# A two-layer attention and mixture-of-experts kernel: expert-owned table rows, routing by groups of tiles, and attention units in pairs

## The chip, the cores and the metric

The kernel runs on one core of one Trainium2 chip. The metric is the device time of one execution in microseconds (us). The core has a matrix engine (TensorE, "PE"; its weight loads are shown apart as "PEld"), a vector engine (DVE), a scalar engine (ACT), a general engine (POOL), and a sync engine (SP) that here only issues transfers. Each engine works through its own list of instructions in order, and waits on semaphores for the others.

## The reference, cut to what matters

All data is fp32. The input is x (8 batches of 100 tokens, width 512) and a context (8 batches of 722 rows, width 512). Two layers follow each other, each a cross attention and a mixture of eight experts.

```python
x = x + L0_xattn(layernorm(x), ctx)   # 16 heads of 32, causal: only context rows 0..99 count
x = x + L0_ffn(layernorm(x))          # gate over 8 experts, top 2, GELU, 512 -> 2048 -> 512
x = x + L1_xattn(layernorm(x), ctx)   # 16 heads of 64; keys and values: own 100 tokens and 722 context rows
x = x + L1_ffn(layernorm(x))          # router over 8 experts, top 2, SwiGLU, 512 -> 1024 -> 512, layernorm of the sum
```

In L1_xattn the keys and the values of the context are the same projection, `memories @ Wm`:

```python
mem = split_heads(memories @ Wm)
k = concatenate([k, mem], axis=2); v = concatenate([v, mem], axis=2)
out = einsum(softmax(einsum(q, k) * scale), v)
```

An expert computes only the tokens that chose it: a token has two experts, so each layer sends 1600 rows to experts.

## The kernel before, in words

The 800 tokens lie in seven tiles of 128 rows, the last of 32. The stages run one after the other, PE first in each.

**Weights.** The class `Weights` (L44-64) streams 1 MB pieces through a pool of eight buffers, in a fixed order, all on SP's queue; `get(k, ahead)` asks for piece k and lets later ones start.

**a0, the first attention.** 32 units, one for each of four column chunks and eight batches; projections of the next chunk's columns stand between the units, so the last chunk's eight units have none. While it runs, SP fills two DRAM tables, `sent` and `answers`, with zeros in pieces of 512 KB. Then an output loop over the seven tiles adds the projection to x, normalises each tile, and computes its router logits (`logits0`).

**Routing of the first layer.** After the last tile's logits `two_largest` (L188) finds both experts of all tokens at once, and `places` (L218) ranks the tokens for each expert by a matmul with a triangle of ones. It sorts the experts by their number of tokens into eight slots with capacities of 256 to 176 rows. Since a slot's rows start at a fixed place, a token's row is known only when all totals are known. `send` (L303-308) then issues 14 indirect DMAs on POOL (7 tiles, 2 experts each) that write rows of x into `sent`. While they run, `project_early` (L435) computes five units' context projections of the second attention (batch 0) and stores them in DRAM: `context_columns` (L406-415) makes `mT` by 16 matmul instructions, and `context_rows` (L417) transposes it to `mv`.

**FFN0.** Per slot, `arrived` (L322-329) reads up to 256 rows from `sent`, transposes them, `hidden0` (L656) and `products` (L341) multiply, `returned` (L353-363) writes rows to `answers`.

**Between the layers.** PE first projects five early units of batch 1; then POOL fetches two answers for each tile (`fetch`, L315), the sum is made, and after that the tiles are normalised and transposed one by one (a second loop), and q, k and v are multiplied (L400, L813).

**a1, the second attention.** 64 units: a unit is one batch b and one pair of heads ic. In unit n, PE projects the context for the unit (`keys` and `values`; a kept unit reloads it from DRAM on SP's queue instead), computes scores (`weighed`, L752), turns unit n-1's probabilities (`turned`, L773-779) and multiplies them with the values (`attended`, L794). DVE takes the row maximum (L756), ACT the exponential with its sum (L758), DVE the reciprocal of the sums (L763). POOL copies that to a [100,128] tile `wide` (L782), PE transposes it (L788), ACT copies the transpose, and DVE multiplies with it (L797).

**Output and routing of the second layer.** After the last unit: seven output projections (L840, L843), then normalisation (L118-140), transposes (L151) and logits (L166) of the seven tiles, then `two_largest`, `places` and 14 sends as before, the reading from `sent` (L329), and FFN1 (L884). The kernel ends with 14 fetches, a weighted sum, the layernorm and the store.

Of the kernel before, what the change touches and what calls it, by code (L numbers as in the profile page):

```python
# [13 lines left out]
P = 128  # L14
# [17 lines left out]
EARLY = ((0, 1, 3, 5, 7), (0, 1, 3, 5, 7))  # L32
KEPT = {(b, ic): (b * len(EARLY[0]) + k) for b in range(len(EARLY)) for k, ic in enumerate(EARLY[b])}


CAPS = (256, 240, 228, 220, 204, 200, 184, 176)
STARTS = tuple(sum(CAPS[:s]) for s in range(NE))
CAP = CAPS[0]
OVER = NT - CAPS[-1]
ROWS = sum(CAPS) + NE * OVER  # L40
# [3 lines left out]
class Weights:  # L44


    def __init__(self, nc, pool, pieces):
        self.nc, self.pool, self.pieces, self.tiles = nc, pool, pieces, []

    def load(self, n, behind=None):  # L50

        while len(self.tiles) < min(n, len(self.pieces)):
            t = self.pool.tile([P, 4, 512], F32, tag="w", name=f"w{len(self.tiles)}")
            piece = self.pieces[len(self.tiles)]
            if behind is not None:
                self.nc.gpsimd.tensor_copy(t[:1, 0, :1], behind[:1, 0, :1])
            self.nc.sync.dma_start(out=t, in_=piece() if callable(piece) else piece)
            self.tiles.append(t)
# [7 lines left out]
def two_layers(ctx: ExitStack, tc: tile.TileContext, a: dict, out: bass.AP):  # L66
# [8 lines left out]

    pieces = [a[n] for n in ("k_w", "q_w", "v_w", "o_w")]
    W_L0F = len(pieces)
# [8 lines left out]
    pieces += [a["Wq"][g] for g in range(2)] + [a["Wkv"][g] for g in range(4)]  # L86
    pieces += [a["Wm"][g] for g in range(2)] + [a["Wo"][g] for g in range(2)]
# [74 lines left out]
    def router_logits(lg, i, xT, wg, bg, psum, tag):  # L162
        w, t0 = rows[i], i * P
        ps = psum.tile([P, NE], F32, tag=tag, name="ps_lg")
        for dc in range(DC):
            nc.tensor.matmul(  # L166
                ps[:w], xT[:, dc, t0 : t0 + w], wg[:, dc, :], start=dc == 0, stop=dc == DC - 1 and bg is None
            )
        if bg is not None:
            nc.tensor.matmul(ps[:w], ones[:, :w], bg, start=False, stop=True)  # L170
        nc.vector.tensor_copy(lg[:w, i, :], ps[:w])

    def over_experts(t):
        return t.unsqueeze(2).to_broadcast([P, NTILE, NE])

    def largest(v, pool, name):

        m = pool.tile([P, NTILE], F32, tag=f"m_{name}", name=f"m_{name}")
        nc.vector.tensor_reduce(m, v, AX.X, ALU.max)
        at = pool.tile([P, NTILE, NE], F32, tag=f"at_{name}", name=f"at_{name}")  # L180
        nc.vector.tensor_tensor(at, v, over_experts(m), ALU.is_equal)
        nc.vector.tensor_tensor(at, at, rank.unsqueeze(1).to_broadcast([P, NTILE, NE]), ALU.mult)
        first = pool.tile([P, NTILE], F32, tag="first", name=f"first_{name}")
        nc.vector.tensor_reduce(first, at, AX.X, ALU.max)
        nc.vector.tensor_tensor(at, at, over_experts(first), ALU.is_equal)
        return m, at

    def two_largest(v, below, pool, name):  # L188
        m1, at1 = largest(v, pool, f"{name}1")
        rest = pool.tile([P, NTILE, NE], F32, tag="rest", name=f"rest_{name}")  # L190
        nc.vector.scalar_tensor_tensor(rest, at1, below, v, ALU.mult, ALU.add)
        m2, at2 = largest(rest, pool, f"{name}2")
        return m1, at1, m2, at2
# [8 lines left out]
    places_of = const.tile([P, 3, NE], F32, name="places_of")  # L202
    count = const.tile([P, NE], F32, name="count")
    for s in range(NE):
        nc.vector.memset(count[:, s : s + 1], float(s))
        for k, n in enumerate((STARTS[s], CAPS[s], sum(CAPS) + s * OVER - STARTS[s] - CAPS[s])):
            nc.vector.memset(places_of[:, k, s : s + 1], float(n))

    def row_of(s, r):
        return STARTS[s] + r if r < CAPS[s] else sum(CAPS) + s * OVER + r - CAPS[s]  # L210

# [3 lines left out]
    kept_keys = dram.tile([len(KEPT), P, S], F32, name="kept_keys")  # L215
    kept_values = dram.tile([len(KEPT), P, NSC, P], F32, name="kept_values")

    def places(at1, at2, pool, psum, tag, name):  # L218

        sel = pool.tile([P, NTILE + 1, NE], F32, tag="sel", name=f"sel_{name}")  # L220
        nc.vector.memset(sel[:, NTILE - 1 :, :], 0.0)
        nc.vector.tensor_tensor(sel[:, : NTILE - 1, :], at1[:, : NTILE - 1, :], at2[:, : NTILE - 1, :], ALU.add)
        nc.vector.tensor_tensor(
            sel[:LAST, NTILE - 1, :], at1[:LAST, NTILE - 1, :], at2[:LAST, NTILE - 1, :], ALU.add
        )
        before = pool.tile([P, NTILE + 1, NE], F32, tag="before", name=f"before_{name}")
        nc.vector.memset(before[:, 0, :], 0.0)
        for i in range(NTILE):
            nc.vector.tensor_tensor(before[:, i + 1, :], before[:, i, :], sel[:, i, :], ALU.add)
        ps = psum.tile([P, NTILE + 1, NE], F32, tag=tag, name=f"ps_rank_{name}")  # L230
        nc.tensor.matmul(ps, every, before, start=True, stop=False)
        nc.tensor.matmul(ps, upper, sel, start=False, stop=True)
        tot = ps[:, NTILE, :]
        square = [P, NE, NE]
        key = pool.tile([P, NE], F32, tag="key", name=f"key_{name}")
        nc.vector.scalar_tensor_tensor(key, tot, float(NE), rank, ALU.mult, ALU.add)
        hot = pool.tile(square, F32, tag="hot", name=f"hot_{name}")
        nc.vector.tensor_tensor(
            hot, key.unsqueeze(1).to_broadcast(square), key.unsqueeze(2).to_broadcast(square), ALU.is_gt
        )  # L240
        slot = pool.tile([P, NE], F32, tag="slot", name=f"slot_{name}")
        nc.vector.tensor_reduce(slot, hot, AX.X, ALU.add)
        nc.vector.tensor_tensor(
            hot, slot.unsqueeze(2).to_broadcast(square), count.unsqueeze(1).to_broadcast(square), ALU.is_equal
        )
        three = [P, 3, NE, NE]
        wide = pool.tile(three, F32, tag="wide", name=f"wide_{name}")
        nc.vector.tensor_tensor(
            wide, hot.unsqueeze(1).to_broadcast(three), places_of.unsqueeze(2).to_broadcast(three), ALU.mult
        )  # L250
        mine = pool.tile([P, 3, NE], F32, tag="mine", name=f"mine_{name}")
        nc.vector.tensor_reduce(mine, wide, AX.X, ALU.add)
        all_ = [P, NTILE, NE]
        over = pool.tile(all_, F32, tag="over", name=f"over_{name}")
        nc.vector.tensor_tensor(over, ps[:, :NTILE, :], mine[:, 1:2, :].to_broadcast(all_), ALU.is_ge)
        nc.vector.tensor_tensor(over, over, mine[:, 2:3, :].to_broadcast(all_), ALU.mult)
        where = pool.tile(all_, F32, tag="where", name=f"where_{name}")
        nc.vector.tensor_tensor(where, ps[:, :NTILE, :], mine[:, 0:1, :].to_broadcast(all_), ALU.add)
        nc.vector.tensor_tensor(where, where, over, ALU.add)
        out = []  # L260
        for k, at in enumerate((at1, at2)):
            pick = pool.tile([P, NTILE, NE], F32, tag="pick", name=f"pick{k}_{name}")
            nc.vector.tensor_tensor(pick, at, where, ALU.mult)
            place = pool.tile([P, NTILE], F32, tag="place", name=f"place{k}_{name}")
            nc.vector.tensor_reduce(place, pick, AX.X, ALU.add)
            whole = pool.tile([P, NTILE], mybir.dt.int32, tag=f"whole{k}", name=f"whole{k}_{name}")
            nc.vector.tensor_copy(whole, place)
            out.append(whole)
        who = pool.tile(square, F32, tag="who", name=f"who_{name}")
        nc.vector.tensor_tensor(  # L270
            who, hot.rearrange("p e s -> p s e"), count.unsqueeze(1).to_broadcast(square), ALU.mult
        )
        first = pool.tile([P, NE], F32, tag="firsts", name=f"firsts_{name}")
        nc.vector.tensor_reduce(first, who, AX.X, ALU.add)
        experts = pool.tile([P, NE], mybir.dt.int32, tag="experts", name=f"experts_{name}")
        nc.vector.tensor_copy(experts, first)
        much = pool.tile([P, NE], F32, tag="much", name=f"much_{name}")
        nc.vector.tensor_tensor(much, tot, mine[:, 1, :], ALU.is_gt)
        most = pool.tile([P, 1], F32, tag="most", name=f"most_{name}")
# [725 lines left out]
```

## Time and profile before

| what | value |
|---|---|
| median of three runs | 1883.63 us (1882.03 to 1885.28) |
| the profiled execution | 1887.75 us |
| its span | 1886.0 us |
| mean TensorE clock granted | 0.952 of full speed |
| PE busy | 1744.2 us, 92% of the span |
| DVE, ACT, POOL busy | 576.5, 468.3, 161.7 us |
| moved by DMA | 225.15 MB, mean 119 GB/s |

The profile is one execution; "busy" is the time in which an engine had an instruction at work. The stages lie in its span as follows, in us: a0 from 0 to about 170, its outputs and the logits to 207, routing to 255, FFN0 to 640, between the layers to 698, the products of q, k and v and the attention units to 1448, outputs and routing to 1550, FFN1 and the end to 1886. In tables by window, each engine has its busy time and, in parentheses, its number of instructions; then come the granted clock, the share of busy DMA engines and the GB/s. A time line row gives start, duration, engine, line, operation and tiles, and in brackets the idle time before it with what ended it.

### The profile page before, as it was taken

The numbers are of one execution on the slowest core, as the hardware profiler recorded it, in microseconds if no ns is written. First come the engines' busy times: TensorE is split into PE (matmuls) and PEld (weight loads), VectorE is DVE, ScalarE is ACT, GpSimd is POOL, SyncE is SP. The second block draws the span as 40 slices with busy tenths as digits, with TensorE's granted clock in tenths as the row PEclk, the third lists the DMA queues.
The fourth block names the chain that finished last, engine by engine and source line by source line (L and its number), as shares of the span: only waits on it lengthen the run. The fifth ranks groups of instructions, "written<-read, shape, count | busy, mean of one in ns | idle before, by whom it ended". The sixth has DMA issues, their size and how long they took to land. (4 is left out here: it accounts for less than half of the span.)

```text
span 1886.0 us, 26129 instructions
## 1 busy us (share of the span) xinstructions
PE 1744.2 (92%) x10442; PEld 1318.2 (70%) x10442; DVE 576.5 (31%) x1379; ACT 468.3 (25%) x1389; POOL 161.7 (9%) x281
## 2 busy tenths in 40 slices
PE   5999969999999879999999999999999939999990
PEld 2455559999999745666666666666666428999990
DVE  4465300101111140355444234444443321111115
ACT  2374311111111141343333323333332010010110
POOL 4010110000000130000000000000000140000003
PEclk9997879999999979999999999999999859999995
DMA  9701284464556552032000000000000056555523
GB/s 368 313 24 55 108 317 164 177 248 174 201 205 231 196 176 79 24 95 72 1 32 1 32 1 32 1 33 1 1 1 1 12 199 224 183 181 203 206 89 113
DMA packets 51883, 225.15 MB, mean 119 GB/s; under 512 B 8336, under 2 KB 10008, under 8 KB 35104
## 3 DMA queue, kind: packets, MB, share of 16 engines
q1 hardware_dynamic: 32440, 169.51, 24.8%
q0 software_dynamic: 10064, 32.15, 4.8%
q10 hardware_dynamic: 9240, 21.65, 3.2%
q8 instruction: 86, 1.41, 0.3%
q14 instruction: 53, 0.43, 0.1%
HBM read 176.76 MB, written 46.53 MB: 118 GB/s over the span
## 5 line engine op out<-in xcount | busy, mean ns | idle before, releaser
L341 PE MATMUL ps_y<-h,w 128*128 128x256 f32 (+7 forms) x1536 | 280.5, 344 | 0.0
L411 PE MATMUL ps_m<-cb,w 128*128 128x361 f32 x864 | 277.6, 472 | 0.0
L341 PEld LDWEIGHTS ps_y<-h,w 128*128 128x128 f32 x1536 | 268.6, 190 | 7.9
L411 PEld LDWEIGHTS ps_m<-cb,w 128*128 128x128 f32 x864 | 158.9, 189 | 95.4 <-issue 3.6
L656 PE MATMUL ps_h<-xgT,w 128*128 128x256 f32 (+7 forms) x1024 | 189.9, 347 | 0.0
L656 PEld LDWEIGHTS ps_h<-xgT,w 128*128 128x128 f32 x1024 | 181.0, 192 | 6.0
L758 ACT ACTIVATE pr<-ps_sc,m 100x822 f32<-100x822 f32 x128 | 120.0, 943 | 192.6 <-DVE m L756 192.6
L774 DVE COPY prT<-ps_ptA 128x500 f32<-128x500 f32 x128 | 82.2, 678 | 197.1 <-PE ps_ptA L773 197.1
L756 DVE TENSOR_REDUCE m<-ps_sc 100x1 f32<-100x822 f32 x128 | 123.8, 1009 | 47.2 <-PE ps_sc L752 47.2
L660 ACT ACTIVATE h<-ps_h,s_b 128x256 f32<-128x256 f32 (+7 forms) x128 | 56.2, 439 | 315.6 <-PE ps_h L656 315.6
L415 ACT COPY mT<-ps_m 128x361 f32<-128x361 f32 x128 | 59.0, 462 | 252.1 <-PE ps_m L411 224.3
L400 PE MATMUL ps_col<-xT,w 128*128 128x400 f32 x320 | 115.3, 519 | 0.0
L884 PE MATMUL ps_g<-xgT,w 128*128 128x256 f32 (+7 forms) x512 | 104.6, 348 | 0.0
L884 PE MATMUL ps_u<-xgT,w 128*128 128x256 f32 (+7 forms) x512 | 103.1, 344 | 0.0
L400 PEld LDWEIGHTS ps_col<-xT,w 128*128 128x128 f32 x320 | 61.9, 197 | 46.2 <-issue 4.6
L884 PEld LDWEIGHTS ps_g<-xgT,w 128*128 128x128 f32 x512 | 91.4, 192 | 3.0
L884 PEld LDWEIGHTS ps_u<-xgT,w 128*128 128x128 f32 x512 | 91.1, 191 | 2.8
L752 PE MATMUL ps_sc<-mT,qT 64*100 64x311 f32 (+1 forms) x512 | 91.9, 466 | 0.0
L889 ACT ACTIVATE sg<-ps_g 128x256 f32<-128x256 f32 (+7 forms) x64 | 22.3, 349 | 239.3 <-PE ps_g L884 239.3
L782 POOL COPY wide<-sums 100x128 f32<-100x128 f32 x64 | 18.8, 294 | 728.1 <-DVE sums L763 728.1
L890 DVE TENSOR_TENSOR h<-ps_u,sg 128x256 f32<-128x256 f32 (+7 forms) x64 | 24.4, 381 | 184.2 <-PE ps_u L884 152.9
L794 PE MATMUL ps_av<-prT,mv 128*64 128x100 f32 (+1 forms) x1536 | 80.6, 253 | 0.0
(240 smaller groups left out, 1964.0 us busy)
## 6 DMA issues: line engine op xcount, KB each, us to landing
w<-in_W SPq DMA_DIRECT2D x64, 1024.0 KB
w<-in_w_gate SPq DMA_DIRECT2D x16, 1024.0 KB
w<-in_w_up SPq DMA_DIRECT2D x16, 1024.0 KB
w<-in_w_down SPq DMA_DIRECT2D x16, 1024.0 KB
sent<-nil SPq DMA_DIRECT2D x25, 512.0 KB
cb<-in_ctxT ACTq DMA_DIRECT2D x8, 1444.0 KB
answers<-nil SPq DMA_DIRECT2D x19, 512.0 KB
xg<-sent POOLq DMA_DIRECT2D x18, 256.0 KB, 4.8
```

The costliest lines, as they stand in the source:

```text
L341: nc.tensor.matmul(py[:, k, :n], ws[f // 4][:, f % 4, dc * P : (dc + 1) * P], h[:, f, :n], start=f == 0, stop=f == nf - 1,)
L400: nc.tensor.matmul(ps[:, :HALF], w[c // 4][:, dc, (c % 4) * P : (c % 4 + 1) * P], xT[:, dc, cols], start=dc == 0, stop=dc == DC - 1,)
L411: nc.tensor.matmul(pm[:, : S // 2], w_m[ic // 4][:, dc, (ic % 4) * P : (ic % 4 + 1) * P], cb[:, dc, h * (S // 2) : (h + 1) * (S // 2)], st ...
L415: nc.scalar.copy(mT[:, h * (S // 2) : (h + 1) * (S // 2)], pm[:, : S // 2])
L656: nc.tensor.matmul(ph[:, :n], w[:, dc, j * P : (j + 1) * P], xg[:, dc, :n], start=dc == 0, stop=dc == DC - 1,)
L660: nc.scalar.activation(h[:, f, :n], ph[:, :n], AF.Gelu, bias=b1s[:, e, f : f + 1])
L752: nc.tensor.matmul(sc[:, bank, c0:c1], qT[r, ic, q0 : q0 + T], keys_, start=True, stop=True)
L756: nc.vector.tensor_reduce(m, sc[:, :, :NKH], AX.XY, ALU.max, negate=True)
L758: nc.scalar.activation(pr.rearrange("p (a n) -> p a n", a=2), sc[:, :, :NKH], AF.Exp, bias=m, accum_out=sums[:, j : j + 1],)
L774: nc.vector.tensor_copy(prT[:, : NSC - 1, :], pt)
L794: nc.tensor.matmul(po[r, 0, :], vj, prT[j][:w, c, :], start=c == 0, stop=c == NSC)
L884: nc.tensor.matmul(p_[:, :n], w_[:, dc, j * P : (j + 1) * P], xg[:, dc, :n], start=dc == 0, stop=dc == DC - 1,)
```

## The change

Six things are changed at once.

1. **Rows of the tables.** Each expert owns 800 rows of `sent` and `answers`: a token's row is expert times 800 plus its rank. A table has 6400 rows in place of 6700, and both are zero-filled whole, in 50 pieces (before, the main part of `answers` was left out: 44 pieces). The slots read their expert's rows by an address from a register, which POOL loads as well as SP.
2. **Routing by groups.** A class `Route` chooses, ranks and sends by groups of tiles: (0-2), (3-4), (5-6) in the first layer, (0-1), (2-3), (4), (5-6) in the second. `order()` sorts the experts into slots after the last group. One group's work is about 20 short DVE instructions, two rank matmuls and two sends for each tile.
3. **Early projections.** 14 units are kept in place of ten: all eight of batch 0, six of batch 1. Those of batch 0 are a generator of 24 steps: one step in each of the last ten iterations of a0's loop, six in its output loop, eight after `order()`. Wm and the context for them come through the weight pool ahead of the zero fill of `answers`. In the second attention the kept units are reloaded on POOL's queue.
4. **Between the layers.** Each tile is normalised and transposed as soon as its answers are added, in one loop. The weight order is Wq, Wm, Wkv, Wo.
5. **Attention units in pairs.** Units of batches 0 and 2, then of 1 and 3, alternate (kept, not kept); batches 4 to 7 follow in order. `wide` and its transposes are gone: SP writes the reciprocals to DRAM (100x2 numbers, transposed) and reads them back twice, spread over 64 partitions each. The multiply (L822) is placed one unit later on DVE, right behind the next unit's reciprocal (L787) and ahead of its copies of turned probabilities (L802).
6. **Outputs within the attention.** Output projection, normalisation, logits and the group's routing of tiles 0 to 4 are placed after units 33, 35, 37, 50 and 58; those of tiles 5 and 6 follow the last unit.

```diff
-EARLY = ((0, 1, 3, 5, 7), (0, 1, 3, 5, 7))
+EARLY = ((0, 1, 2, 3, 4, 5, 6, 7), (0, 1, 3, 5, 6, 7))
-ROWS = sum(CAPS) + NE * OVER
+ROWS = NE * NT
+GROUPS = ((0, 3), (3, 5), (5, NTILE)), ((0, 2), (2, 4), (4, 5), (5, NTILE))
...
+        def group(self, i0, i1, xn):
+            g, v = i1 - i0, self.logits[:, i0:i1, :]
+            at1 = self.largest(v, self.m[0][:, i0:i1], 1)
...
+            at2 = self.largest(other, self.m[1][:, i0:i1], 2)
...
+            nc.tensor.matmul(ps[:, : g + more, :], every, self.before[:, i0 : i1 + more, :], start=True, stop=False)
+            nc.tensor.matmul(ps[:, :g, :], upper, self.sel[:, i0:i1, :], start=False, stop=True)
+            row = self.temp([P, NTILE, NE], "row")[:, :g, :]
+            nc.vector.tensor_tensor(row, ps[:, :g, :], base.unsqueeze(1).to_broadcast([P, g, NE]), ALU.add)
...
+            for i in range(i0, i1):
+                for k in range(2):
+                    d = nc.gpsimd.indirect_dma_start(
+                        out=sent, out_offset=bass.IndirectOffsetOnAxis(ap=self.where[k][: rows[i], i : i + 1], axis=0),
+                        in_=xn(i)[: rows[i], :], in_offset=None,
+                    )
...
+    def rows_of(table, layer, s, r, n):
+        of_all = table.rearrange("(e r) d -> e r d", e=NE)
+        return of_all[bass.ds(owner[layer][s], 1), r : r + n, :].rearrange("o r d -> (o r) d")
...
-            nc.gpsimd.dma_start(out=xg[:w, s, :], in_=sent[row : row + w, :])
+            nc.gpsimd.dma_start(out=xg[:w, s, :], in_=rows_of(sent, layer, e, r0 + s * P, w))
...
+        fill(sent)
+        weights.load(W_L0F)
+        fill(answers)
...
         for n in range(len(units) + 2):
+            if n >= len(units) - B:
+                next(steps)
...
             if i > 0:
                 logits0(i - 1)
+                next(steps)
         logits0(NTILE - 1)
+        route.order(lambda: weights.load(W_L0F + 2))
+        for _ in steps:
+            pass
...
+            xn = fw.tile([P, D], F32, tag="y", name="xn1")
+            scaled(xn, x[:, i, :], *factors(moments(x[:, i, :], "a1"), "b", twice=True))
+            to_columns(xT1, xn, i * P, rows[i], ps, gamma1, beta1)
+            nc.gpsimd.tensor_tensor(x[:, i, :], x[:, i, :], bo, ALU.add)
...
-                nc.sync.dma_start(out=mT, in_=kept_keys[KEPT[b, ic]])
+                nc.gpsimd.dma_start(out=mT, in_=kept_keys[KEPT[b, ic]])
...
             nc.vector.reciprocal(sums, sums)
+            share, over = shares[b * IC + ic], aw.tile([P, T], F32, tag="share", name="over1", bufs=4)
+            nc.sync.dma_start(out=share.rearrange("j t -> t j"), in_=sums)
+            for r, j in zip(rows_, range(2)):
+                nc.sync.dma_start(out=over[r], in_=share[j].partition_broadcast(H1))
...
-            wide = small.tile([T, 2, H1], F32, tag="wide", name="wide1")
-            nc.gpsimd.tensor_copy(wide, sums.unsqueeze(2).to_broadcast([T, 2, H1]))
...
-            nc.tensor.transpose(po[:, 1, :], wide.rearrange("t j d -> t (j d)"), ident[:T, :T])
...
-            nc.scalar.copy(over, po[:, 1, :])
-            nc.vector.tensor_tensor(qT[:, ic, b * T : (b + 1) * T], po[:, 0, :], over, ALU.mult)
+            mine = qT[:, ic, b * T : (b + 1) * T]
+            nc.scalar.copy(mine, po)
+            return lambda: nc.vector.tensor_tensor(mine, mine, over, ALU.mult)
...
+        units = [(b + 2 * k, ic) for b in range(2) for ic in range(IC) for k in range(2)]
+        units += [(b, ic) for b in range(4, B) for ic in range(IC)]
...
+            if divide is not None:
+                divide()
+            if before is not None:
+                divide = attended(*before[:4], *turn)
+            before = here
+            if n in due:
+                output(due[n])
+        divide()
+        attended(*before[:4], *turned(*before[4]))()
+
+        for i in range(NTILE):
+            if i not in due.values():
+                output(i)
+        route.order(lambda: weights.load(W_L1F + 2))
```

## The prediction

> **What bounds the kernel now.** I read the page first: busy shares, then the slices in tenths.
>
> ```profile
> PE 1744.2 (92%) x10442; PEld 1318.2 (70%) x10442; DVE 576.5 (31%) x1379; ACT 468.3 (25%) x1389; POOL 161.7 (9%) x281
> ...
> PE   5999969999999879999999999999999939999990
> ...
> PEclk9997879999999979999999999999999859999995
> ```
>
> TensorE (PE) is the bound. 1886.0 - 1744.2 = 142 us of the span are PE idle, in few places: the start, slices 5 and 6 (routing), 13 and 14 (between the layers), 32 and 33 (second routing), the end. Work that moves between other engines counts only there; elsewhere only PE work that vanishes counts. Next, windows of 20 us at those places and inside the attention:
>
> ```profile
> 240.00:260.00 20.00, 7.64 (x23) 6.24 (x24) 2.64 (x8) 1.76 (x2) 5.74 (x14) 0.50 0.78 292
> 680.00:700.00 20.00, 8.80 (x31) 6.24 (x32) 8.04 (x21) 11.36 (x35) 8.72 (x7) 0.58 0.15 51
> 1000.00:1020.00 20.00, 20.00 (x152) 13.56 (x151) 9.14 (x18) 7.20 (x22) 0.59 (x2) 1.00 0.00 1
> 1520.00:1540.00 20.00, 0.31 (x2) 0.12 (x1) 3.57 (x22) 0.00 (x0) 12.47 (x13) 0.50 0.64 239
> ```
>
> PE is solid at 1000-1020 and nearly empty at 1520-1540, with the clock at half. The time line there names the holder, POOL's sends, one each 1.28 us, and the chain of waits goes on to FFN1:
>
> ```profile
> 1523.88 1.02 POOL L308 DMA_INDIRECT sent<-xnf,whole_f  x1 [11.94 <-DVE pick_f L263]
> ...
> 1540.41 0.86 POOL L308 DMA_INDIRECT sent<-xnf,whole_f  x1 [0.30 <-issue]
> ```
>
> ```profile
> 1543.20 2.91 DMA xg<-sent
> ...
> 1550.00 2.13 PE ps_g L884 x5
> ```
>
> From the last send's end (1541.27) to FFN1 (1550.00) are 8.73 us. In the attention, POOL's `wide` copies date the reciprocals, and the PE rows price what goes:
>
> ```profile
> 839.19 0.29 POOL L782 COPY wide<-sums 100x128 f32<-100x128 f32 x1 [11.78 <-DVE sums L763]
> 846.18 0.29 POOL L782 COPY wide<-sums 100x128 f32<-100x128 f32 x1 [6.70 <-DVE sums L763]
> 853.97 0.29 POOL L782 COPY wide<-sums 100x128 f32<-100x128 f32 x1 [7.49 <-DVE sums L763]
> 937.88 0.29 POOL L782 COPY wide<-sums 100x128 f32<-100x128 f32 x1 [9.93 <-DVE sums L763]
> 948.10 0.29 POOL L782 COPY wide<-sums 100x128 f32<-100x128 f32 x1 [9.92 <-DVE sums L763]
> ```
>
> ```profile
> 1002.93 0.31 PE L788 MATMUL ps_av<-ident,wide 100*128 100x100 f32 x1
> 1003.16 1.25 PE L794 MATMUL ps_av<-prT,mv 128*64 128x100 f32 x24
> ```
>
> A unit that is not kept takes 948.10 - 937.88 = 10.22 us. A kept one with one that is not takes 853.97 - 839.19 = 14.78, in steps of 6.99 and 7.79. So a kept unit costs 4.56, that is 5.66 us less. The transpose lasts 0.31 but holds the stream for about 0.2 (the next matmul starts 0.23 after it).
>
> **What the Trainium skill says.** "TensorE: Matmul & The Clock Gate", Part 1: after an idle window of some 3.4 us PE falls to half clock, and needs about as long busy to come back. The windows agree in kind (0.50 at 1520-1540, 1.00 at 1000-1020). The same page, "Architectural detail": ACT and DVE take their instructions strictly in order; so an early instruction that waits holds all behind it. The trace of before has no case that I rest on. "DMA: Bandwidth & Descriptors", "Anatomy of one DMA": about 2 us of each transfer are fixed, mostly the confirmation of the write; its rules for kernel authors say that a strided last dimension becomes one descriptor per element. The trace has only larger transfers (`back<-answers` 3.8 us median, `xg<-sent` 4.8), which lie above it.
>
> **The change part by part.** Sums are against the profiled execution (1887.75, span 1886.0, so 1.75 lies around it); the median is 1883.63, 4.1 lower, and I take the difference over.
>
> *First routing and its fill-ins.* Before: logits done 206.96, first FFN0 matmul 255.00, 48 us, of which five early units fill about 30. An early unit is some 5.9 us of PE (16 L411 matmuls 5.1, transposes 0.9). Ten of 24 steps go into a0's last iterations, 3 and a third units, 20 us; there PE is busy throughout but at clock 0.52, the units being chains of short work (3.03 us each, against about 2.8 with column matmuls between), so I take 9 as hidden: +12 (bounds 0 and +20). Six steps in the output loop, 11.7 us, in iterations whose PE is busy 4.65 of 5 us: +10 (+5 to +12). Groups' waits of DVE and rank matmuls: +3. Logits end at about 232. The last group then needs 2.8 (choice) + 0.7 (rank) + 2.6 (rows), four sends of 1.28 = 5.1, and 8.73 to FFN0: 20 us, in which the last eight steps (15.6) are hidden. FFN0 starts at 252: -3 (range -10 to +8), with three more units done. Filling 50 pieces in place of 44 adds 3 MB of SP transfers under a0; hidden, the DMA share there being low by 140 us, and if not, the context for the steps comes ahead of the second fill anyway. The stores' queue on SP holds nothing urgent but `order()`'s register loads, long after.
>
> *Address registers.* One more register operation on POOL for each of 36 row transfers: nothing under FFN0's solid PE, 0.3 us ahead of the first `xg`.
>
> *Between the layers.* Before, the last `ps_y` ends at 639, q's first matmul is at 697.84. Fetching ends at 673, then a second pass of seven tiles. With normalisation and transposes in the fetch loop, after the last fetch only one tile's chain (about 3 us for the sum and norm, 2 for transposes and copies, and 7 for weights and the start) is left: q at 685, -13 (-5 to -18). The sixth early unit lies in the wait for fetches. If the fetches are late, it is this chain that is late, equally.
>
> *Attention.* 64 transposes by 0.2 = -13 (0 to -15). Four more kept units by 5.66 = -22.6; their reloads pass from SP to POOL's queue, where nothing else stands in the attention but sends of groups. The second context of a pair is loaded when a buffer comes free, one unit ahead: +4 (0 to +5).
>
> *The new wait.* Reciprocal, write of 200 single numbers, read back, multiply. On SP the reads wait behind the write; on DVE the multiply stands behind the next unit's reciprocal; behind it are the copies of turned probabilities, for which PE's `attended` waits. No row shows such a transfer: from below twice 2 us = 4 us by the skill's price, an estimate; from above two of `xg<-sent`, 2 x 4.8 = 9.6. I take 6.5. It may last the spacing of reciprocals, 6.99 at the least, plus about 2 us of slack until the copies matter: 9. So nothing; at 9.6 it is 28 units by 0.6 = +17. With that cover gone each further us costs a us per unit.
>
> *Outputs and the second routing.* Before: 1448.4 (last `attended`) to 1550.0, 101.6 us. After, behind the last unit: output 5 6.4, norm 3.05 (from the matmul's end at 1454.72 through add, statistics, root, scaling), transposes and router 2.5; output 6 6.9, norm 3.05, 1.7; choice 3.4, rank and rows 2.1, four sends 5.1, 8.73 + 0.3: 43 us. In the attention, outputs 0 to 4: 5 x (6.9 + 1.7) + 3 x 0.7 = 45 us of PE, and waits, since PE meets the transposes two score products after the output: each 3.45 less what covers it, 17; rank matmuls wait for some 3.1 in two groups, 6; 1 more. 43 + 45 + 24 = 112 against 101.6: +11 (0 to +25; a falling clock after such waits is in the upper end). POOL's seven bias adds ahead of the last sends lie under the tail's chain.
>
> *FFN0, FFN1, tail.* Same instructions and sizes: 0.
>
> Sum: -3 - 13 - 13 - 22.6 + 4 + 11 = -36.6. In the profile 1887.75 - 36.6 = 1851; in the median 1883.63 - 36.6 = 1847.
>
> **The rivals.** *A, slower: the shares come too late.* If the round trip is 11 us, each pair takes 2 x (11 - 2) = 18 in place of 14.78 us: 14 pairs cost 45, more than all gains; median 1892. It decides from about 10.3 us, where the pairs cost 14 x 2.6 = 36. For it: single-number writes of which this profile has no measure, and a write that must be confirmed before each read. Against: the DMA share of 0.00 in the attention, so the queues are empty; and all shown transfers, much larger, take under 5.
>
> *B, the outputs' waits cost their double.* Each wait of 3 us and more lets the clock fall, and the next several us run at half: 5 x 4 = 20 more, median 1867. For it: 0.50 at 1500-1520, where just these norms and transposes run. Against: single waits of 3 us lie near the window's length.
>
> *C, the waits are covered.* Scores, context matmuls and other tiles cover the 24 us, and a0's steps fill only stretched time: -24, median 1823. For it: PE's clock of 0.52 in a0's tail, half of whose time could be taken without loss. Against: PE's order is fixed, and it meets the transposes early.
>
> *D, nothing is won in routing at all.* Early units merely move, and the first layer gives back +8 in place of -3, the gap between the layers -5: median 1866; it adds to B or A rather than deciding a sign.
>
> **How the numbers follow.** My own case, 1833 to 1866 and centred on 1847: 0.46. C, below: 0.11. B and D, up to 1880: 0.13. Within 0.2% (1879.9 to 1887.4, what this measurement can just tell from no change): 0.03. A, and any wait of its kind at the new places, above: 0.27. So faster 0.70, same 0.03, slower 0.27. The range, 1816 to 1898, leaves out some 0.05 below and 0.14 above, A's dearer half.
>
> **What would show it.** Right: L752 to L819 follow each other without L788's row; the spacing in pairs stays at about 14.4; DVE's row for L822 has little idle before it, put to a DMA; FFN0 starts at about 252, q about 12 us after the last fetch, and from the last `attended` to FFN1 are some 44 us. Wrong: L822 with hundreds of us of idle before it, and PE idle ahead of L819 (A); clock under 0.9 in the slices with outputs (B); FFN0 later than 260, which would mean that a0 hid nothing; or context matmuls that wait for `cb` at each new pair of batches.

## The result, and the profile after

The changed kernel is slower: a median of 1972.86 us in four runs (1962.4 to 1979.17) against 1882.83 in four runs of the kernel before; the ratio is 1.0471, with a 95% interval of 1.0423 to 1.0519. The forecast was 1847. The profiled execution is the shortest of the four, 1962.4 us with a span of 1960.9, so the times read from it lie some 10 us under the median. First its page, the same lines as shown of before:

```profile
PE 1755.8 (90%) x10398; PEld 1320.0 (67%) x10398; DVE 590.0 (30%) x1450; ACT 484.2 (25%) x1412; POOL 168.6 (9%) x263
...
PE   5999889999999789787998998999899939999990
...
PEclk9999889999999989898999898899899969999995
```

Counted from 0, there are new dips of PE where it was solid before: slices 16 to 18, 21, 24 and 28, all in the second attention, with a lower clock beside most of them. The old dips (5, 13, 14, 32) are still there. To see how much, I cut the span at five marks that both kernels have, and set the forecast's own steps beside them (us; the forecast is before plus the sum's terms for that stretch; e1, e4, e10 and e14b are experiments told below).

| stretch | before | forecast | after | e1 | e4 | e10 | e14b |
|---|---|---|---|---|---|---|---|
| start to the first FFN0 matmul | 255.0 | 252 | 253.7 | 253.7 | 250.4 | 253.8 | 254.0 |
| to the first q matmul | 442.8 | 430 | 444.2 | 443.1 | 443.5 | 443.1 | 442.6 |
| to the 32nd reciprocal (the paired units) | 370.1 | 345 | 408.7 | 344.1 | 344.6 | 344.1 | 338.3 |
| to the 64th reciprocal (single units, with outputs 0 to 4 where they are moved) | 377.0 | 440 | 456.2 | 461.3 | 442.9 | 377.6 | 370.0 |
| to the first FFN1 matmul | 104.9 | 46 | 59.5 | 58.4 | 49.6 | 97.8 | 99.7 |
| to the end of the span | 336.2 | 336 | 338.6 | 340.0 | 338.8 | 337.6 | 339.8 |

Of the 111 us between forecast and profile, 64 lie in the paired units, 16 in the stretch with the outputs, 14 between the layers, 13 behind the last unit, the small rest at the start and the end.

The view of waits by engine and line of the kernel after, limited to DVE, names a wait that the kernel before does not have (total us, number of times, longest). Limited to PE, it names what follows from it:

```profile
DVE qT L822 <- DMA over<-shares: 105.2, 31, 8.5
```

```profile
PE ps_mv L437 <- DVE prT L802: 40.5, 12, 5.6
```

Of the 105.2 us, 79.9 lie in the paired stretch.

SP's time line in the paired units shows where it comes from. L789 is the issue of a write of reciprocals, L791 the two reads, which SP may issue only when the write has landed:

```profile
854.99 0.28 SPq L789 DMA_DIRECT2D shares<-sums  x1
862.51 1.08 SPq L791 DMA_DIRECT2D over<-shares  x2
863.69 1.11 SPq L789 DMA_DIRECT2D shares<-sums  x1
871.16 1.08 SPq L791 DMA_DIRECT2D over<-shares  x2
873.65 0.28 SPq L789 DMA_DIRECT2D shares<-sums  x1
881.41 1.27 SPq L791 DMA_DIRECT2D over<-shares  x2
```

From the issue of a write to that of its reads are 7.5 to 7.8 us here (5.5 to 9.6 over the 32 paired units, 7.1 on average), and the write of the unit at 861.51 waits on SP behind the reads of the unit before. DVE and PE in the same place:

```profile
861.51 0.17 DVE L787 RECIPROCAL sums<-sums 100x2 f32<-100x2 f32 x1 [1.11 <-ACT pr L782]
866.60 0.26 DVE L822 TENSOR_TENSOR qT<-qT,over 128x100 f32<-128x100 f32 x1 [4.92 <-DMA over<-shares]
866.78 1.26 DVE L802 COPY prT<-ps_ptA 128x500 f32<-128x500 f32 x2
```

```profile
863.54 0.66 PE L437 MATMUL ps_mv<-ident,mT 128*128 128x128 f32 x4
867.50 0.44 PE L437 MATMUL ps_mv<-ident,mT 128*128 128x128 f32 x2 [3.31 <-DVE prT L802]
867.87 0.42 PE L776 MATMUL ps_sc<-kT,qT 64*100 64x100 f32 x4
868.13 2.21 PE L776 MATMUL ps_sc<-mT,qT 64*100 64x311 f32 x8
```

DVE has its reciprocal at 861.51 and then stands at the multiply L822 until 866.60; the copies L802, which it could have made from about 863 on (PE's transposes for them are done then), come after it; PE waits 3.31 us for them. Then the scores take 2.21 us in place of 1.39, at a granted clock of 0.60 (868.1 to 870.4). This is the chain that rival A described, at its place.

In the single units the write is faster, but not fast:

```profile
1303.38 0.28 SPq L789 DMA_DIRECT2D shares<-sums  x1
1308.71 1.08 SPq L791 DMA_DIRECT2D over<-shares  x2
```

It takes 5.3 us from issue to issue here, 5.8 in the median of the last 32 units. The units are 10.0 us apart, and the multiply finds its shares ready.

### The profile page after: what moved, and what is told of

It reads as the page before. It is cut to its first block, busy times and chain, and to the rows that moved or that the text cites. A ratio compares the mean times of both kernels' runs of the same rounds, so it can differ in the third digit from the quotient of the medians.

```text
span 1960.9 us, 26528 instructions
## 1 busy us (share of the span) xinstructions
PE 1755.8 (90%) x10398; PEld 1320.0 (67%) x10398; DVE 590.0 (30%) x1450; ACT 484.2 (25%) x1412; POOL 168.6 (9%) x263
## 4 chain that ended last, share of the span: by engine, by line
PE 42%; issue 34%; DMA 16%; DVE 4%; ACT 2%; SPq 1%; POOL 0%; POOLq 0%; another core or an unknown queue 0%; ACTq 0%; DVEq 0%
PE ps_m L425 13%; PE ps_col L414 7%; DMA answers<-y 6%; DMA shares<-sums 5%; PE ps_sc L776 3%; PE ps_v L847 3%; PE ps_av L819 3%; PE ps_o L865 2%; PE ps_mv L437 2%; PE ps_ptA L801 2%; DMA over<-shares 2%; PE ps_v L516 1%; DMA back<-answers,where 1%; PE ps_o L621 1%; ACT pr L782 1%
## 5 line engine op out<-in xcount | busy, mean ns | idle before, releaser
L425 PE MATMUL ps_m<-cb,w 128*128 128x361 f32 x896 | 307.0, 493 | 0.0
L425 PEld LDWEIGHTS ps_m<-cb,w 128*128 128x128 f32 x896 | 172.6, 199 | 102.8 <-issue 17.1
L802 DVE COPY prT<-ps_ptA 128x500 f32<-128x500 f32 x128 | 81.8, 677 | 149.6 <-PE ps_ptA L801 149.5
L819 PEld LDWEIGHTS ps_av<-prT,mv 128*64 128x64 f32 (+1 forms) x1536 | 74.7, 146 | 50.7 <-issue 48.5
L437 PE MATMUL ps_mv<-ident,mT 128*128 128x128 f32 (+1 forms) x384 | 64.0, 295 | 49.1 <-DVE prT L802 40.5
L776 PE MATMUL ps_sc<-mT,qT 64*100 64x311 f32 (+1 forms) x512 | 102.7, 517 | 0.0
L819 PE MATMUL ps_av<-prT,mv 128*64 128x100 f32 (+1 forms) x1536 | 88.4, 266 | 4.7 <-DVE prT L802 4.2
L437 PEld LDWEIGHTS ps_mv<-ident,mT 128*128 128x128 f32 (+1 forms) x384 | 41.6, 142 | 64.3 <-DVE prT L802 43.9
```

The source lines that it names most:

```text
L425: nc.tensor.matmul(pm[:, : S // 2], w_m[ic // 4][:, dc, (ic % 4) * P : (ic % 4 + 1) * P], cb[h][:, dc, : S // 2], start=dc == 0, stop=dc = ...
L437: nc.tensor.transpose(pt[:w, c - c0, :], mT[:, c * P : c * P + w], ident)
L776: nc.tensor.matmul(sc[:, bank, c0:c1], qT[r, ic, q0 : q0 + T], keys_, start=True, stop=True)
L802: nc.vector.tensor_copy(prT[:, : NSC - 1, :], pt)
L819: nc.tensor.matmul(po[r, :], vj, prT[j][:w, c, :], start=c == 0, stop=c == NSC)
```

## The experiments

My theory after the result: the share round trip makes the paired stretch long (A); the outputs inside the attention wait for their own norms and choice and pull the clock down (B). The rival to A was that the pairing itself does it: late contexts, or reloads on POOL's queue. The rival to B was that outputs are cheap there and only shares are at fault. In every verdict "before" is the kernel before on the same chip.

### e1: shares as before, all else changed

```diff
-            nc.sync.dma_start(out=share.rearrange("j t -> t j"), in_=sums)
-            for r, j in zip(rows_, range(2)):
-                nc.sync.dma_start(out=over[r], in_=share[j].partition_broadcast(H1))
-            return prs, over
+            return prs, sums
...
+            nc.gpsimd.tensor_copy(wide, sums.unsqueeze(2).to_broadcast([T, 2, H1]))
...
+            nc.tensor.transpose(po[:, 1, :], wide.rearrange("t j d -> t (j d)"), ident[:T, :T])
```

> The changed kernel with one part undone: the reciprocals are spread as before (POOL copy, PE transpose, multiply behind the value products), nothing goes through DRAM. If the share round trip is what stretched the paired units, the time from the first q matmul to the 32nd reciprocal falls from 408.7 to about 350 us, the single units cost 0.2 us more each again, and the whole comes to 1905 to 1925. If the outputs inside the attention or the pairing itself (contexts loaded late, reloads on POOL) hold it, the paired stretch stays near 400 and the whole above 1950.

Measured: 1900.89 us, ratio 1.0086 (1.0057 to 1.0115). The paired stretch is 344.1 us, its reciprocals 7.8 and 7.0 us apart as before. That is better than expected (about 350, and 1905 to 1925 for the whole). So the pairing, the late contexts and POOL's reloads cost nothing; with four more kept units the stretch is 26.0 us shorter than before, where 22.6 were forecast for them. The shares cost 65 us there. Windows over the paired stretch, of the changed kernel and of e1, show in what form:

```profile
697.87:1106.58 408.71, 363.51 (x2343) 229.75 (x2344) 136.33 (x249) 120.10 (x344) 22.35 (x42) 0.92 0.32 53
```

```profile
696.79:1040.93 344.14, 344.13 (x2374) 220.71 (x2375) 136.71 (x249) 120.19 (x344) 31.55 (x73) 0.99 0.19 59
```

PE idles for 45 us where e1 has no idle time at all, and it is busy 19 us longer though it makes 32 transposes less, at a clock of 0.92. The waits are two thirds of the cost; the slow clock behind them is the rest.

The five outputs cost as much as in the changed kernel: the stretch of single units is 461.3 against 377.6 in e10, which has none in it: 84 us.

### e2: the shares through DRAM in the kernel before

The same lines moved into the kernel before, with the multiply one unit later.

> The kernel before with one part done alone: reciprocals through DRAM, multiply one unit later. If the round trip is the cause, the units of batches 2 to 7 (10.22 us apart, more than a trip of 9.4) run without a wait at about 10.0, and only the 20 short spacings of batches 0 and 1 are stretched, by 2 to 4 us each second one: net 1875 to 1900. If the trip costs nothing by itself, the 64 transposes are simply gone: 1870. If SP or the DMA engines are slowed as a whole, every unit is longer than 10.2 and it is over 1910.

Measured: 1924.76 us, ratio 1.0223 (1.0204 to 1.0242). By its time that is the third case, over 1910; by its units it is the first, only dearer. The single units are 9.98 us apart, the 0.24 us of a transpose less, as expected. But the stretch of batches 0 to 3 takes 414.6 us against 370.1, with spacings up to 19.9 in batches 0 and 1. In this kernel the kept units' reloads stand on SP's queue too, behind reads that wait for writes, so that two waits add; I had not counted the queue. The run shows that the trip alone, on this queue, costs 44 us; it does not separate the two waits.

### e3 and e4: where the outputs stand

e3 is e1 with all seven projections behind the last unit and the rest tile by tile; e4 is e1 with an output in three steps:

```diff
-            if n in due:
-                output(due[n])
+            for k, step in enumerate((output, logits, grouped)):
+                if n - k in due:
+                    step(due[n - k])
```

> As e1_wide, and all seven output projections behind the last unit, followed by norms, logits and groups tile by tile. If the five outputs inside the attention cost their 86 us (measured in the changed kernel as longer spacings) mostly in waits, this is 35 to 55 us faster than e1_wide: 1860 to 1880. If the outputs inside the attention are cheap and only the shares were at fault, it is slower than e1_wide by 10 us or more.

> As e1_wide, but an output is cut in three: the projection with add and norm after its unit, transposes and logits after the next unit, choice, ranks and sends after the one behind that. The waits for the norm and the choice lie under a unit each. If the waits are the cost, each of the five outputs adds 8 to 10 us in place of about 17, the clock stays at 1.00 there, and the whole comes to 1860 to 1875, below e3. If the cost is the work itself or the clock, it stays within 10 us of e1_wide.

Measured: e3 1877.90 us, ratio 0.9975 (0.9963 to 0.9987); e4 1870.18, ratio 0.9933 (0.9909 to 0.9957). Both times lie within what was expected if B holds. But e3 gains 23 us on e1 and not 35 to 55: it wins 84 in the attention, and its end, tile by tile, is 64 us longer (122.0 against 58.4). PE's time line of e1 shows one output inside the attention:

```profile
1122.37 7.13 PE L865 MATMUL ps_o<-w,qT 128*128 128x512 f32 x16
1129.43 0.42 PE L776 MATMUL ps_sc<-kT,qT 64*100 64x100 f32 x4
1132.53 0.66 PE L157 MATMUL ps_tp<-ident,xnf 128*128 128x128 f32 x4 [2.68 <-DVE xnf L146]
1133.92 1.35 PE L173 MATMUL ps_lg<-p_w_router,xTf 128*128 128x8 f32 x8 [0.73 <-ACT xTf L159]
1138.31 0.58 PE L252 MATMUL ps_rank<-before,every 128*128 128x16 f32 x2 [3.04 <-DVE before L249]
1138.73 0.59 PE L253 MATMUL ps_rank<-sel,upper 128*128 128x16 f32 x2
1139.16 7.88 PE L425 MATMUL ps_m<-cb,w 128*128 128x361 f32 x16
```

The waits are 2.68 + 0.73 + 3.04 = 6.45 us. The granted clock is 0.50 from 1134.5, after the first two of them, to 1144.8, and the 16 context matmuls that follow take 7.88 us where they take 5.13 elsewhere: 2.75 us for the clock. In the changed kernel the window with an output at 1200 to 1220 has a clock of 0.75. Windows over the stretch of single units, of e1 and of e10, split the whole cost:

```profile
1040.93:1502.24 461.31, 437.43 (x2751) 280.37 (x2750) 177.62 (x395) 142.03 (x383) 19.22 (x42) 0.96 0.04 13
```

```profile
1041.06:1418.63 377.57, 376.62 (x2599) 247.10 (x2598) 154.30 (x297) 125.22 (x363) 9.39 (x32) 1.00 0.03 9
```

PE idles 23 us more with outputs than without, and is busy 61 us more. For 32 us of its busy time in e1 the clock stands at 0.50, which is worth 16; so the five outputs are 23 us of waits, 16 of slow clock and some 45 of work. In e4 PE works on a unit in between, and the stretch falls from 461.3 to 442.9, still 65 above e10: there 10 us are waits and 8 are the clock. What is left in e4 above the work is thus about half of what e1 had; an output costs 13.1 us and not the 8 to 10 that were expected.

### e5, e9 and e13b: what makes the write slow

e5 writes the same 200 numbers as 100 runs of two, read in the old places, so that shares come in a wrong order. e9 writes one head's 100 numbers singly and reads them for both heads. e13b lays them out token by token and reads both heads at once:

```diff
+            nc.sync.dma_start(out=share, in_=sums)
+            nc.sync.dma_start(out=over, in_=share.partition_broadcast(P))
...
+                for j in range(2):
+                    r = slice(j * H1, (j + 1) * H1)
+                    nc.vector.tensor_tensor(mine[r], mine[r], over[r, :, j], ALU.mult)
```

> The changed kernel, with the 100x2 reciprocals written as 100 runs of two numbers in place of 200 single ones (the reads are the same, so the shares come in a wrong order: the attention's weights are not the reference's). If the number of single runs sets the length of the write, the time from the write's issue to the reads' issue in the quiet units falls from 5.5 to 3.5 to 4.5 us, and the paired stretch from 408.7 to about 390, the whole to 1945 to 1960. If the time is a fixed latency, it stays at 5.5 and the whole at 1960 to 1980.

> The changed kernel, with the reciprocals of one head of the pair alone written (100 single numbers in place of 200) and read twice, so the second head is divided by the first one's sums: its output is not the reference's. If the number of runs is what the write takes its time for, its 5.5 us in quiet units fall to about 2.9 as with 100 runs of two, and the whole to about 1895. If the 4-byte size is what is slow, they fall to no less than 4.5, and the whole stays above 1920.

> The changed kernel, with the reciprocals of a unit laid out token by token in DRAM (100 runs of two numbers), read back by one transfer to all 128 partitions, and the multiply split in two by head. If the 4-byte runs of the write are the cause, the write takes about 2.9 us as in e5, the paired stretch from the first q matmul to the 32nd reciprocal is 340 to 350 us in place of 408.7, and the whole 1885 to 1900. If e5 was fast for its wrong order alone, or the larger read takes its place, it stays over 1920.

Measured: e5 1893.63 us, ratio 1.0048 (1.0031 to 1.0065), over 50 us less than expected, with a paired stretch of 342.0 in place of about 390. e13b 1889.96, ratio 1.0033 (1.0015 to 1.0052), as expected. SP's time line in single units, of e5, of e9 and of e13b:

```profile
1301.16 0.28 SPq L789 DMA_DIRECT2D shares<-sums  x1
1304.16 1.08 SPq L791 DMA_DIRECT2D over<-shares  x2
```

```profile
1299.65 0.28 SPq L789 DMA_DIRECT2D shares<-sums  x1
1305.19 1.08 SPq L791 DMA_DIRECT2D over<-shares  x2
```

```profile
1306.83 0.30 SPq L789 DMA_DIRECT2D shares<-sums  x1
1309.83 0.32 SPq L790 DMA_DIRECT2D over<-shares  x1
```

3.0, 5.5 and 3.0 us; in the median of the last 32 units 3.0, 5.9 and 3.0. A hundred single numbers take as long as two hundred (5.8), a hundred runs of two take 3.0: the number of runs is not what counts, the 4-byte run is. So the first of e9's two cases fell. (e9's whole time, 3168.39 us, ratio 1.6815 (1.6781 to 1.6848), says nothing on this: its wrong shares send so many rows to some experts that the overflow work of FFN1 runs, with 15326 PE instructions in place of 10398.) With pairs of numbers, e13b's waits for the shares fall from 105.2 to 22.8 us, and its paired stretch to 337.5, below e1's 344.1: of this trip PE feels nothing (it idles 0.1 us in the stretch), and the transposes are saved.

What I can't tell apart is whether a run of 4 bytes is slow as such, or because neighbouring ones lie side by side in DRAM; no run spread them out.

### e6 and e7: between the layers, and the last choice

e6 is e1 with batch 1's early stores issued by SP in place of ACT. e7 is e1 with the seven additions of the final bias on POOL held back by a small copy that waits for the last `where`.

> As e1_wide, with the stores of batch 1's early units on SP's queue in place of ACT's. If ACT, which waits at these stores with the tiles' norms and column copies behind it, is why nothing was won between the layers, the first q matmul comes 5 to 8 us sooner than 696.8 (689 to 692) and the whole is that much under e1_wide: 1893 to 1896. If PE's early projections or the fetches set that start, nothing moves.

> As e1_wide, with the seven bias additions on POOL held back until the last rows are chosen. If they slow DVE's choice of the last group (8.7 us from logits to rank matmul in e1_wide, single instructions of 1 us in place of 0.2), it takes about 4 us and the time from the last reciprocal to FFN1 falls from 58.4 to 51 to 54: 1894 to 1897. If not, it stays at e1_wide's 1901.

Measured: e6 1895.68 us, ratio 1.0065 (1.0046 to 1.0083), which looks like a gain on e1. But from the first FFN0 matmul to the first q matmul it takes 443.0 us, e1 443.1. The difference came ahead of FFN0, whose start lies between 250.2 and 254.0 in kernels that are alike up to there; so a few us between whole times say nothing, and the stretches are compared instead. The theory that ACT's stores hold this start fell. e7: 1891.62, ratio 1.0042 (1.0028 to 1.0056); from the last reciprocal to FFN1 50.3 us in place of 58.4. DVE's choice in the changed kernel, and in e7, with three of its instructions each:

```profile
1600.36 1.19 DVE L230 TENSOR_TENSOR at<-at,rank 128x16 f32<-128x16 f32 x1
1601.47 1.29 DVE L920 TENSOR_TENSOR m<-m,m 128x7 f32<-128x7 f32 x1
1602.68 0.16 DVE L232 TENSOR_REDUCE first<-at 128x2 f32<-128x16 f32 x1
```

```profile
1530.89 0.17 DVE L230 TENSOR_TENSOR at<-at,rank 128x16 f32<-128x16 f32 x1
1530.98 0.16 DVE L921 TENSOR_TENSOR m<-m,m 128x7 f32<-128x7 f32 x1
1531.10 0.17 DVE L232 TENSOR_REDUCE first<-at 128x2 f32<-128x16 f32 x1
```

While POOL adds (1594.1 to 1602.7 in the changed kernel), instructions of 0.17 us on DVE take up to 1.3. In this choice those that were slowed all read two tensors; those that read one, like L232, keep their 0.17.

### e8: a diagonal in place of the identity

A try at a better kernel: the share is multiplied in as the probabilities are turned (a plain matmul with a diagonal of reciprocals), outputs in a row, bias late, early stores on SP.

```diff
-                    nc.tensor.transpose(pt[:, c, :], pr[:, T + c * P : T + (c + 1) * P], ident[:T, :T])
+                    nc.tensor.matmul(pt[:, c, :], pr[:, T + c * P : T + (c + 1) * P], diag[:, j, :], start=True, stop=True)
```

> The parts that held, together: expert-owned rows, groups, early units and pairs as changed; the share is multiplied in as the probabilities are turned (a matmul with a diagonal of reciprocals in place of the identity, no wide copy, no DRAM); outputs back to back behind the last unit with norms, logits and groups after them as before; bias additions late, early stores on SP. From the parts: before 1883, units 64 x 0.22 = -14, four more kept -22, outputs and routing 104.9 less ten sends of 1.28 = -12, between the layers -6: about 1830 (1820 to 1840). If the diagonal matmuls cost PE more than the transposes (each 0.1 us), it is 1850 or more.

Measured: 1952.54 us, ratio 1.0358 (1.0341 to 1.0375). A miss, by over 110 us: the single units are 11.56 us apart. Of e8, and of e1 for comparison, the five chunks of one head:

```profile
1001.72 1.25 PE L800 MATMUL ps_ptA<-diag,pr 100*128 100x100 f32 x10
```

```profile
1146.88 0.59 PE L797 MATMUL ps_ptA<-ident,pr 100*128 100x100 f32 x5
```

Five plain fp32 matmuls are ten PE instructions and take 1.25 us; five transposes are five and take 0.59.

### e10, e11, e12 and e14b: the end, and a faster kernel

e10 is e1 with outputs in a row behind the last unit, then norms, logits and groups of all tiles, and the bias late. e11 is e4 with the bias late. e12 is e10 with the first two weight pieces of FFN1 taken from expert 0 and loaded early, whatever the order, so that one slot computes partly with wrong weights. e14b is e10 with e13b's shares.

> As e1_wide (shares by POOL copy and PE transpose), with the end of e8: outputs in a row behind the last unit, norms, logits and groups after them, bias additions late. The last reciprocal to FFN1 took 105.3 us in e8, against 142.1 for the same work in e1_wide (83.7 in the attention, 58.4 behind it): 1901 - 37 = 1864 (1858 to 1870). If e8's slow units were not due to the diagonal matmuls alone, it is over 1880.

> As e4_outputs_staged, with the bias additions held back as in e7. If their costs are apart, e4's 1870 less e7's 9 is 1861 (1857 to 1865). If e4's end hides the choice in another way, 1868 to 1872.

> As e10, with the first two weight pieces of FFN1 taken from expert 0 whatever the order of the experts, and loaded ahead of the outputs (so one slot uses partly wrong weights). If the 2 MB that can only be asked for when the order is known are now late, because so few sends are left behind it, FFN1 starts 4 to 8 us sooner than in e10: 1856 to 1860. If the reading of the sent rows sets the start by itself, it is within 2 us of e10.

> As e10_outputs_row, with the shares through DRAM as in e13b in place of the POOL copies and PE transposes. 64 transposes of 0.22 us go, 14 us, less some waits of short-spaced units (e5 had 27 us of them on DVE, of which few reached PE): 1843 to 1850 against 1855.5. If a round trip still costs the pairs more than the transposes did, it is 1856 or more.

Measured: e10 1855.51 us, ratio 0.9852 (0.9835 to 0.9868). e11 1866.08, 0.9905 (0.9888 to 0.9921). e12 1852.90, 0.9829 (0.9812 to 0.9846). e14b 1845.48, 0.9797 (0.9780 to 0.9813), the fastest, with outputs where the kernel before had them. e14b came as expected; e10 and e12 are a few us below their ranges, e11 is one us above its. The outputs' five places in the attention lose: from the 32nd reciprocal to FFN1 the kernel before takes 481.9 us, e10 475.4, e11 489.0, e4 492.5, e1 519.7. Behind the last reciprocal the late bias wins 5.3 us in e11 (44.3 against e4's 49.6) and 8.1 in e7, so it and the staging overlap in part. In e12 FFN1 starts 3.7 us sooner than in e10, just short of the 4 to 8 expected. On POOL's time line 3.3 us of that lie between the last send and the reading, where its wait falls from 5.10 to 1.82:

```profile
1504.88 0.18 POOL L917 CAST bias<-where 1x1 f32<-1x1 int32 x1
1510.17 1.17 POOL L344 DMA_DIRECT2D xg<-sent  x2 [5.10 <-issue]
```

```profile
1504.27 0.18 POOL L918 CAST bias<-where 1x1 f32<-1x1 int32 x1
1506.27 1.17 POOL L344 DMA_DIRECT2D xg<-sent  x2 [1.82 <-issue]
```

The first is e10, the second e12. With ten sends out of the way, the loads that need the experts' order, asked for at 1504.3 in e10, and the reading share the same moment. How a load on SP's queue delays POOL's issue is not shown by the profile and stays open.

## Why the prediction was wrong

**The step that failed: the new wait.** It was priced at nothing: 6.5 us for the round trip, bounded by 4 and 9.6, against a cover of 9. For the last unit, with quiet queues, write to multiply takes 9.4 us (1563.00 to 1572.36), at the upper bound. In the pairs it is 7.1 us on average from write to reads and mostly 4 to 5 from reads to multiply, about 12.9 in the median from reciprocal to multiply (873.46 to 886.40 is one), outside the bound. The queue adds to it: SP issues a write only after the reads of the unit before, so that with a write of 7.6 us a unit can't be shorter than about 8.7 there, and before the mean spacing in such a pair was 7.4. The bound was taken from `xg<-sent`, a read of long rows; a write of single numbers has no row that answers to it, and its length did not go with its bytes (e5 writes the same bytes in 3.0). "DMA: Bandwidth & Descriptors", "Anatomy of one DMA", from which the lower bound of twice 2 us came, describes transfers that GpSimd issues, and these are SP's; its 2 us are far from the 4-byte write, and the 8-byte write of 3.0 us is nearer to them. The same page's "Rules for kernel authors", with one descriptor per element for a strided last dimension, points at the right line, but e9 shows that the count isn't the measure here.

One thing would have given more cover. The change was meant to place the multiply one unit later on DVE, but in the trace it stands where L797 stood before, right behind the next unit's reciprocal. A place one reciprocal further on would cover some 7 us more; no run tried it, and SP's 8.7 us would have remained.

**Rival A** named the mechanism and the place, with a chance of 0.27 for all of its kind. Its price for a trip of 11 us, 45 over the pairs, is what PE idled there (45.2); the slow clock behind the waits, which A left out, brought the rest of the 65. One sum of A does not come out: by its own formula a trip of 10.3 us costs 14 x 1.8 = 25, and the 36 that were given to it need 10.7.

**Outputs and routing.** Work of 45 us and waits of 24 were taken, and measured are some 45 and 23; the five outputs cost 84 (e1 less e10). What was left out, or rather left to rival B at 20 us, is the clock: 16. Here each single wait is shorter than the window of some 3.4 us that "TensorE: Matmul & The Clock Gate", Part 1 gives, but two follow each other with little work between, and the clock falls before the third begins. In the pairs a single wait of 3.31 us did it too (0.50 from 868.55 on). The end was forecast at 43 us behind the last value product and took 56.4 (1565.93 to 1622.30): from the last logits to the rows 9.8 us, where e7 needs 4.2 (POOL's additions, which I had placed under the tail's chain, held DVE), output 6 took 9.45 in place of 6.9 at a mean clock of 0.74, and from the last send to FFN1 11.85 in place of 8.73.

**Between the layers.** A gain of 13 was forecast, none came: 444.2 against 442.8. The step said that behind the last fetch only one tile's chain is left. But in PE's list all seven tiles' transposes stand behind the early projections, and ACT makes 28 column copies of 0.36 us, 10 us, behind them; the root for the norm of later tiles (L137) stands on ACT behind 16 of these copies, and DVE waits 5.08 us for it. PE, ACT and DVE of the kernel after:

```profile
682.44 0.66 PE L437 MATMUL ps_mv<-ident,mT 128*128 128x128 f32 x4 [0.33 <-ACT mT L429]
684.41 1.09 PE L157 MATMUL ps_tp<-ident,xn 128*128 128x128 f32 x8 [1.31 <-ACT mv L439]
...
696.00 0.60 PE L157 MATMUL ps_tp<-ident,xn 32*128 32x32 f32 x4 [0.94 <-DVE xn L146]
697.87 2.37 PE L414 MATMUL ps_col<-xT,w 128*128 128x400 f32 x3 [1.28 <-ACT xT L166]
```

```profile
685.27 5.70 ACT L166 ACTIVATE xT<-ps_tp,p_ln_b,p_ln_g 128x128 f32<-128x128 f32 x16 [0.59 <-PE ps_tp L157]
690.77 0.57 ACT L137 ACTIVATE rb<-mv_a,eps 128x1 f32<-128x1 f32 x2
```

```profile
691.18 0.16 DVE L140 RECIPROCAL rb<-rb 128x1 f32<-128x1 f32 x1 [5.08 <-ACT rb L137]
```

From the first transpose to q are 13.5 us, before 13.2. The only gain is the sixth unit, which fits in. This is read from the trace; no run changed the order.

**What held.** The first routing: 253.7 against 252 forecast, with three more units done. Four more kept units and the saved transposes: the paired stretch is 337.5 in e13b, where PE hardly waits for shares, against 345 forecast. The single units are 10.0 us apart against 10.22, 0.22 saved as priced. FFN0, FFN1 and the end are as before within 3 us.

## What to carry to other kernels

A small transfer on a path is priced by its own shape: before trading 0.2 us of a busy engine for a trip through DRAM, find a row with runs as short as these, and count the queue behind which the next one waits, not only its length. Work put into the middle of a solid stage brings its waits with it, and the waits bring a slow clock; other work between its steps in that engine's list took off about half of both here, and the outputs in a row behind the stage were faster still. When sends are taken off the end of a routing, ask what could not be asked for until then: here the weights of experts whose order is the last thing known.

## What the runs showed of the hardware

A write of 100 or 200 single fp32 numbers to DRAM took 5.8 to 5.9 us (median) until a dependent issue with quiet queues, one of 100 runs of two 3.0. Additions of 128x512 on POOL made short DVE instructions up to eight times as long (L920 1.29 us, the same in e7 0.16). Plain fp32 matmuls were two PE instructions each, transposes one (e8). Waits of 2.7 and 0.7 us on PE with little work between were followed by 10.2 us at a clock of 0.50, in which a third wait of 3.0 lies (e1, 1134.5 to 1144.8); after a single wait of 3.31 us it was 0.50 for 3.4 (868.55 to 871.96).
